# A four-block transformer on one core: stripes filled without DRAM, values copied by ScalarE, softmax buffers chosen by need, and the best of twelve orders

## The chip, the core and the metric

The kernel runs on one core of a Trainium2 chip. The time is the device time of one execution in microseconds. The kernel before takes 1323.22 us, the median of three runs (1322.68 to 1323.9). All numbers and matmul operands are 32-bit floats. A core has five engines with queues of their own: TensorE (PE; its weight loads are shown apart, as PEld), VectorE (DVE), ScalarE (ACT), GpSimd (POOL) and SyncE (SP), which here does nothing but issue DMAs.

## What is computed

Eight batches of 512 tokens by 256 features go through four residual blocks, each fed by a layer norm without gain or bias:

1. Attention of 16 heads of 16 features with rotary positions. Keys and values come from a latent of 64 features. A fixed bias by distance is added to the scores before the softmax, and a small gated term is added after it:

```python
q = apply_rope(x @ Wq + bq);  k, v = split((x @ Wkv_down + bkv_down) @ Wkv_up + bkv_up);  k = apply_rope(k)
att = softmax(q @ k.T / sqrt(16) + log_sparse + log(decay + 1e-9))
out = att @ v + 0.2 * sigmoid(q @ mean(k)) * mean(v)
x = x + out @ Wo + bo
```

2. A feed-forward block, 256 to 1024 to 256, with ReLU.
3. A retention block without softmax: `(q k^T * D) v`, with D = 0.96875^(i-j) on and below the diagonal.
4. The same feed-forward block again.

## The kernel before

Everything stays on chip: weights are loaded once, and each batch of x is loaded into one tile `x_b`. PE's work falls into two kinds.

*Steps.* The attention of one batch is 4 groups of 4 heads; each group has 8 items (4 blocks of 128 tokens by 2 pairs of heads), 32 items a batch and 256 in all. Item n appears three times. As a score item (`score_item`, tile `s`) it gives two heads' scores, 128 queries by 512 keys each, into a pair buffer of PSUM (tag `sc`, two buffers of two banks); VectorE takes the row maximum (`reduce_item`, tile `mr`). After eight items `shift` transposes the group's maxima (`mx`), ScalarE negates them (`neg`) and a DMA puts them into a spare row of the query tile, so that the next product subtracts them by itself. LAG steps later the item returns as a probability item (`prob_item`, tile `t`): the transposed scores, less the maxima. `soft_item` applies the exponential on ScalarE (tile `p`, four buffers) and multiplies by the decay table `dec_a` on VectorE or on POOL. Items below EARLY (34) put `t` into two of the three small banks (tag `m`) and take two exponentials of 512 columns; later ones take the pair buffer and one of 1024. PVLAG (2) steps later, every second step, `pv_item` multiplies by the values.

Score and probability matmuls use a 32-row strip of the PE array per head: the tiles `qT` and `kT` hold head h of each group in a stripe of 32 partitions, 16 rows of features, one row for the shift, the rest zeros or ones. Both exist twice, for even and odd batches.

*Units.* All other work is cut into `Unit`s, each a function with an estimated PE time, the engines that follow and their times (`then`), predecessors (`after`), and the first step at which it may go. `front1` and `front2` make the units of a batch before its attention: layer norm (`ln_units`: statistics, 1/sigma on POOL, normalization, transposition `xT`), the latent (`lat`), keys, queries, values (`va`), the means for the gated term (`km`, `mv`, `me`, `ga`). Keys and queries come out of PSUM on VectorE as products with cosine and sine (`half_unit`, tiles `rc` and `rs`); `turn` (L446) adds them on POOL, writes them to the DRAM tiles `dk` and `dq`, and reads them back with one DMA for each head of a group, which gives the stripes their order. The values are written by four VectorE additions that also add their bias (L383). `post_units` divides by the softmax's sums; for batches 1 to 6 it goes through DMAs and a reciprocal (`invert`, `divide`), with planned delays of 4.5 and 5.8 us. `rest` makes the units of the output product (`wo`), the two feed-forward blocks (`up`, `down`, tiles `h_x`/`hx` and `x`) and the retention block (`b`, `bv`, `bs`, `bo`).

*The order.* Instructions are pinned to the program order on each engine. The first batch's front is written out by hand from L814. From L835 a planner runs the rest: it keeps clocks for PE, VectorE, ScalarE and POOL, the times at which PSUM buffers come free, and at each turn either issues the next step or a unit from one of the waiting chains. A unit is taken when the next step would leave PE idle, when the chains' backlog is over RESERVE (75 us), and as far as a credit that shares the remaining unit work among the remaining steps allows it. LAG is 10. All loads and stores go through SP's queue in program order; only the shift's DMA goes through ScalarE's.

Of the kernel before, what the change touches and what calls it, by code (L numbers as in the profile page):

```python
# [15 lines left out]
P = 128  # L16
# [19 lines left out]
def tile_kernel(  # L36
# [70 lines left out]
    for h in range(2):  # L107
        move(xs[0][:, 2 * h : 2 * h + 2, :], xv[0][:, 2 * h : 2 * h + 2, :])
# [7 lines left out]
    for j in range(2):  # L116
        move(wd_sb[:, :, j, :], wdown)

    wk_in = at.tile([P, NH, 32], F32, tag="p", bufs=4, name="wk_in")
    for j in range(2):  # L120
        move(wk_in[j * LAT : (j + 1) * LAT].rearrange("p h d -> p (h d)"), wk[:, 0, :])
    wq_in = at.tile([P, NC, NH, 32], F32, tag="p", bufs=4, name="wq_in")
    move(wq_in.rearrange("p c h d -> p c (h d)"), wq[:, :, 0, :])
# [4 lines left out]
    for j in range(2):  # L128
        move(wv_sb[j * LAT : (j + 1) * LAT], wv)
    row = keep([P, 2, D], "row")  # L130
    move(row[:, 0, :], rows[0:D].partition_broadcast(P))
    move(row[:, 1, :], rows[2 * D : 3 * D].partition_broadcast(P))
    wqk_in = rs.tile([P, NC, 2, D], F32, tag="big", bufs=1, name="wqk_in")
    move(wqk_in, wb[:, :, 0:2, :])
    bv, b2 = row[:, 0, :], row[:, 1, :]
    move(vec[LAT:, V_BD : V_BD + 1], vecs[:LAT, V_BD : V_BD + 1])
# [10 lines left out]
    dq = [dr.tile([NH, HD, T], F32, tag=f"dq{i}", name=f"dq{i}") for i in range(2)]  # L147
    dk = [dr.tile([NH, HD, T], F32, tag=f"dk{i}", name=f"dk{i}") for i in range(2)]
# [11 lines left out]
    def buffers(i, eng):  # L160
        eng.memset(kT[i], 1.0)
        eng.memset(qT[i], 0.0)
        gps.memset(vaug[i], 1.0)

    def head_mask():
        dve.reduce_sum(hmask, ident.rearrange("p (h d) -> p h d", d=HH), axis=AX.X)
        gps.tensor_scalar(hmask, hmask, 0.5 / T, None, ALU.mult)
        gps.memset(kmean, 0.0)

    def memory_buffers():  # L170
        for i in range(2):
            gps.memset(gates[i], 0.0)
            move(gates[i][NH : NH + 1, :], rope[HD : HD + 1, 0, :])
            gps.memset(mem[i], 0.0)
        gps.memset(bo_row, 0.0)
        move(bo_row[NH : NH + 1, :], rows[D : 2 * D].unsqueeze(0))
        move(bvc, rows[0:D].rearrange("(c p) -> p c", p=P))
        gps.memset(vmean, 0.0)
        gps.memset(vmask, 0.0)
        gps.memset(vmask[:, :, NH : NH + 1], 1.0)  # L180
        for c in range(NC):
            dve.reduce_sum(
                vmask[:, c, c * HH : (c + 1) * HH], ident.rearrange("p (h d) -> p h d", d=HD), axis=AX.X
            )
        gps.tensor_scalar(bvc, bvc, 0.1, None, ALU.mult)

    late = {}

    def late_loads():
        late["dec_a"] = resident(decay_a, "dec_a")  # L190
        xs[1] = load_x(1)

        for g in range(NG):
            at_row = (g % 2) * 4 * HD
            move(wo_sb[at_row : at_row + 4 * HD, g // 2, :], wo.rearrange("(h d) g n -> h d g n", d=32)[:, :HD, g, :])
        late["w1"] = resident(w1, "w1_sb")
        late["w2"] = resident(w2, "w2_sb")

        move(wvu[:, :, :D], wb[:, :, 2, :])
# [13 lines left out]

    wq_sb = keep([P, NC, 2, P], "wq_sb")

    wk_sb = keep([P, P], "wk_sb")
    def regroup():
        for e in range(2):
            half_of = slice(e * HH, (e + 1) * HH)
            act.copy(  # L220
                wk_sb[e * LAT : (e + 1) * LAT, :].rearrange("p (h d) -> p h d", d=HH),
                wk_in[e * LAT : (e + 1) * LAT, :, half_of],
            )
        for e in range(2):
            half_of = slice(e * HH, (e + 1) * HH)
            for c in range(NC):
                act.copy(wq_sb[:, c, e, :].rearrange("p (h d) -> p h d", d=HH), wq_in[:, c, :, half_of])
# [4 lines left out]
    def biases():  # L232
        pick = keep([P, 2, 32], "pick")
        for e in range(2):
# [3 lines left out]
            )  # L238
        ps = misc("qk_bias")
# [6 lines left out]
    NI = B * NG  # L246
    NS = 8 * NI
    LAG, PVLAG = 10, 2
# [19 lines left out]
    def product():  # L268
        ps = misc("ct")
        for c in range(NC):  # L270
            for o in range(NC):
                mm(ps[:, c * D : (c + 1) * D], wr[1][:, o, c * P : (c + 1) * P], wr[0][:, o, :], o == 0, o == NC - 1)
        dve.tensor_copy(ct.rearrange("p c d -> p (c d)"), ps)

    def product_biases():
        both = rs.tile([P, NC], F32, tag="ve", name="both")
        dve.tensor_mul(both, vec[:, V_BQB : V_BQB + NC], vec[:, V_BKB : V_BKB + NC])
        ones = rs.tile([P, P], F32, tag="xn", name="ones")
        gps.memset(ones, 1.0)
        ps = misc("bb")  # L280
        for j, v in ((0, V_BKB), (1, V_BQB)):
            for c in range(NC):
                for o in range(NC):
                    mm(
                        ps[:, 2 * j + c : 2 * j + c + 1], wr[j][:, o, c * P : (c + 1) * P], vec[:, v + o : v + o + 1],
                        o == 0, o == NC - 1,
                    )
        for o in range(NC):
            mm(ps[:, 4:5], ones, both[:, o : o + 1], o == 0, o == NC - 1)
        dve.tensor_copy(bb, ps[:, :5])  # L290
        dve.tensor_copy(wvu[:, :, D], bb[:, 2:4])
# [23 lines left out]
    def ln_units(get, name, pool, bias=None):  # L315
# [39 lines left out]
        for h in range(2):  # L355
            a = Unit(lambda h=h: stats(h), then=(("DVE", 1200), ("POOL", 1000)))
# [802 lines left out]
```

## Time and profile before

| | us |
|---|---|
| Median of three runs | 1323.22 |
| Profiled execution, its own time | 1321.83 |
| Its span, first to last instruction | 1320.0 |
| TensorE busy | 1241.8 (94%) |
| VectorE busy | 798.4 (60%) |
| ScalarE busy | 444.9 (34%) |
| GpSimd busy | 407.7 (31%) |
| Mean granted TensorE clock | 0.979 |

The chain that ended last lies on PE for 81% of the span and on VectorE for 13%. Three things are needed to read the profile. A float32 matmul shows as two passes, so a count of 1024 stands for 512 matmuls. Matmuls on different strips of the array overlap, so the mean duration of one (664 ns for `s`) is more than its share of busy time (297.4 us over 1024). And almost every instruction is issued through one helper for its engine, so lines say little (L69 for VectorE, ScalarE and POOL, L205 for matmuls, L91 for SP's DMAs) and the names of the tiles identify the work.

### The profile page before, as it was taken

Reading aid. Unit: us, or ns where it says so; the run is one execution under the profiler, and the core shown is the slowest. Engines: PE = TensorE matmul, PEld = TensorE weight load, DVE = VectorE, ACT = ScalarE, POOL = GpSimd, SP = SyncE. Lnnn points to the kernel's source line nnn. Section 1 sums busy time; section 2 is a strip of 40 time slices with the busy share of each in tenths; the row PEclk is TensorE's granted clock in tenths of the full one; section 3 lists DMA queues with packets and bytes.
Section 4 is the critical chain, followed back from the end, with each engine's and each line's share of the span. In section 5 each row is a group of like instructions: output and inputs, shape, how many; then the busy total and the mean of one; then the engine's idle time right before and its main releaser. Section 6 shows DMA issues by size and latency. Waiting matters only on the chain.

```text
span 1320.0 us, 15524 instructions
## 1 busy us (share of the span) xinstructions
PE 1241.8 (94%) x5972; PEld 609.7 (46%) x5972; DVE 798.4 (60%) x1300; ACT 444.9 (34%) x634; POOL 407.7 (31%) x461
## 2 busy tenths in 40 slices
PE   6899887989999999989999999999989999999999
PEld 3333232435452554435543455435535454555757
DVE  4587986687666576755766757565665465442320
ACT  2144434433434233332343423333233423332120
POOL 4165454243323233231332333232331223121210
PEclk9599999999998999999999999999989999999999
DMA  5440040022000400022000400013000000000000
GB/s 136 134 75 7 1 86 14 6 49 50 14 5 6 94 21 9 5 53 52 24 5 3 84 29 14 5 31 68 5 9 5 22 9 1 1 17 1 0 4 28
DMA packets 33935, 39.03 MB, mean 30 GB/s; under 512 B 11691, under 2 KB 21292, under 8 KB 33582
## 3 DMA queue, kind: packets, MB, share of 16 engines
q1 hardware_dynamic: 33222, 37.79, 12.4%
q8 instruction: 47, 0.77, 0.2%
q10 hardware_dynamic: 640, 0.26, 0.1%
q14 instruction: 26, 0.21, 0.1%
HBM read 21.65 MB, written 12.78 MB: 26 GB/s over the span
## 4 chain that ended last, share of the span: by engine, by line
PE 81%; DVE 13%; DMA 1%; issue 1%; ACT 1%; POOL 1%; SPq 0%; ACTq 0%; DVEq 0%
PE s L205 18%; PE x L205 17%; PE hx L205 16%; PE pv L205 7%; DVE mr L69 6%; PE wo L205 3%; PE bs L205 3%; DVE p L69 3%; PE bo L205 3%; PE t L205 3%; PE bv L205 2%; PE b L205 2%; PE q L205 1%; PE lat L205 1%; PE ga L205 1%
## 5 line engine op out<-in xcount | busy, mean ns | idle before, releaser
L69 ACT ACTIVATE p<-t 128x1024 f32<-128x1024 f32 (+1 forms) x290 | 264.1, 924 | 540.9 <-PE t L205 494.4
L69 DVE TENSOR_REDUCE mr<-s 128x2 f32<-128x1024 f32 x256 | 312.5, 1222 | 219.7 <-PE t L205 202.5
L69 POOL TENSOR_TENSOR p<-p,dec_a 128x512 f32<-128x512 f32 x182 | 233.3, 1302 | 464.5 <-ACT p L69 397.4
L205 PE MATMUL s<-kT,qT 32*128 32x512 f32 x1024 | 297.4, 664 | 40.0 <-DVE mr L69 35.3
L205 PE MATMUL t<-qT,kT 32*128 32x512 f32 x1024 | 298.2, 649 | 6.1 <-DVE mr L69 5.9
L69 DVE TENSOR_TENSOR p<-p,dec_a 128x512 f32<-128x512 f32 x330 | 231.5, 743 | 23.5 <-ACT p L69 23.2
L205 PE MATMUL x<-w_sb,h_x 128*128 128x256 f32 x1024 | 236.9, 387 | 4.6 <-DVE rs L69 4.6
L205 PEld LDWEIGHTS x<-w_sb,h_x 128*128 128x128 f32 x1024 | 194.3, 193 | 58.7 <-issue 26.9
L205 PEld LDWEIGHTS s<-kT,qT 32*128 32x128 f32 x1024 | 81.5, 189 | 215.2 <-DVE mr L69 101.2
L205 PE MATMUL pv<-p,va 128*32 128x512 f32 x1024 | 148.1, 609 | 3.0 <-DVE p L69 2.7
L69 ACT ACTIVATE h_x<-hx,vec 128x512 f32<-128x512 f32 x128 | 88.0, 688 | 142.3 <-PE hx L205 142.3
L205 PE MATMUL hx<-xT_g,w_sb 128*128 128x512 f32 x256 | 121.6, 613 | 0.7 <-ACT xT_g L69 0.7
L69 DVE TENSOR_TENSOR x<-x,x 128x256 f32<-128x256 f32 x64 | 27.1, 424 | 155.2 <-PE x L205 155.2
L205 PE MATMUL hx<-xT_f,w_sb 128*128 128x512 f32 x256 | 117.9, 601 | 1.9 <-ACT xT_f L69 1.8
L205 PEld LDWEIGHTS t<-qT,kT 32*128 32x128 f32 x1024 | 80.8, 185 | 24.6 <-DVE mr L69 9.2
L205 PEld LDWEIGHTS hx<-xT_g,w_sb 128*128 128x128 f32 x256 | 46.2, 192 | 68.6 <-issue 66.5
L205 PEld LDWEIGHTS hx<-xT_f,w_sb 128*128 128x128 f32 x256 | 45.9, 190 | 60.8 <-issue 52.3
L69 POOL TENSOR_TENSOR x<-x,row 128x256 f32<-128x256 f32 x64 | 47.8, 767 | 51.6 <-DVE xn_f L69 30.6
L205 PEld LDWEIGHTS pv<-p,va 128*32 128x32 f32 x1024 | 22.8, 108 | 80.2 <-issue 40.2
L69 POOL TENSOR_TENSOR rc<-rc,rs 128x512 f32<-128x512 f32 x32 | 43.8, 1390 | 15.1 <-DVE rs L69 15.1
L205 PE MATMUL bs<-xT_r,ret 128*128 128x512 f32 (+3 forms) x128 | 37.2, 440 | 0.0
L69 DVE COPY ret<-bv 128x257 f32<-128x257 f32 x32 | 13.1, 423 | 39.3 <-PE bv L205 39.3
(134 smaller groups left out, 976.0 us busy)
## 6 DMA issues: line engine op xcount, KB each, us to landing
dk<-rc SPq DMA_DIRECT2D x16, 256.0 KB
kT<-dk SPq DMA_DIRECT2D x32, 128.0 KB
dq<-rc SPq DMA_DIRECT2D x16, 256.0 KB
qT<-dq SPq DMA_DIRECT2D x32, 128.0 KB
out_dram<-x SPq DMA_DIRECT2D x32, 128.0 KB
x<-in_x_dram SPq DMA_DIRECT2D x7, 512.0 KB
aT<-num SPq DMA_DIRECT2D x96, 32.0 KB
rec<-d_rec SPq DMA_DIRECT2D x12, 256.0 KB
```

Of the source, the lines that this page charges most:

```text
L69: ins = f(*a, **k)
L205: tc.keep_in_program_order(nc.tensor.matmul(o, lhsT=l, rhs=r, start=start, stop=stop))
```

## The change

- **Stripes.** The DRAM tiles `dq` and `dk` go. Each rotated half (128 partitions: 16 heads by 8 features) is written by one DMA for each group straight into every fourth partition of `qT` or `kT`; the feature rows of a stripe are now its even rows, and the shift row is its row 1. `turn` issues eight such DMAs of 64 KB for keys and eight for queries.
- **Values.** Two ScalarE copies take the values out of PSUM without their bias. Since each row of the softmax sums to one, the bias of the values passes through `Wo` once and is added to `bo_row`.
- **Softmax items.** Below EARLY, an item takes the two small banks only where the plan's time for that is over 0.2 us earlier than the pair buffer's.
- **The first batch's front**, written by hand, has another order: the latent in two halves, `wq` loaded through ScalarE's queue, the next x and the decay table loaded ahead of the stripes, matmuls of the identity (`warm`) at the start and between score-only steps, the bias products of the retention block moved from PE to POOL and ScalarE, and part of the gate's and memory's units moved behind the first scores.
- **The planner** becomes a function that can run without emitting; it is run for four values of `reserve` and three of `later` (which shifts how much work is left for the tail), and the order with the lowest planned end is emitted. The planned end is charged 1.7 us for each planned gap on PE of more than 1.2 us. Several planned times change, among them the delays of the division (7.5 and 12 us), and 6 us for the stripes to land. LAG becomes 12.

```diff
-                move(d[:, e * HH : (e + 1) * HH, :], o)
-            src = d.rearrange("(g s) r t -> s r g t", s=4)
-            to = (qT, kT)[j][b % 2]
-            for h in range(4):
-                move(to[h * 32 : h * 32 + HD], src[h])
+        def stripes(j, g, e):
+            move((qT, kT)[j][b % 2][2 * e : P : 4, g, :], rot[j, e][g * 32 : g * 32 + 32, :])
...
+                rotate(j, e, gps)
+                for g in range(NG):
+                    stripes(j, g, e)
+            if j == 0 and b > 1:
+                move(qT[b % 2][1:P:32], zero_rows)
...
-                for i in range(2):
-                    dve.tensor_tensor(
-                        vaug[b % 2][:, 2 * i + j, : NH * 17].rearrange("p (h d) -> p h d", d=17)[:, :, :HD],
-                        ps[j][:, i * D : (i + 1) * D].rearrange("p (h d) -> p h d", d=HD),
-                        bv.rearrange("p (h d) -> p h d", d=HD),
-                        ALU.add,
-                    )
+                act.copy(
+                    vaug[b % 2][:, j::2, : NH * 17].rearrange("p i (h d) -> p i h d", d=17)[:, :, :, :HD],
+                    ps[j].rearrange("p (i h d) -> p i h d", i=2, d=HD),
+                )
...
+        def bias_through_wo():
+            ps = misc("bo")
+            for c in range(NC):
+                mm(ps[:, :D], vmean[:, c, :], wo_sb[:, c, :], c == 0, c == NC - 1)
+            dve.tensor_add(bo_row[: NH + 1, :], ps[: NH + 1, :D], bo_row[: NH + 1, :])
...
+    RESERVES, LATERS = (45000, 60000, 75000, 90000), (-30000, 0, 30000)
-    LAG, PVLAG = 10, 2
+    LAG, PVLAG = 12, 2
...
-        if n < EARLY:
+        if spare[n]:
...
-        u = [Unit(evacuate, then=(("ACT", 600), (None, 4500)))]
+        u = [Unit(evacuate, then=(("ACT", 600), (None, 7500)))]
-            u.append(Unit(invert, then=(("DVE", 350), (None, 5800)), after=u[-1:]))
+            u.append(Unit(invert, then=(("DVE", 350), (None, 12000)), after=u[-1:]))
...
+    latent(0, 2), latent(1, 2)
+    regroup_k()
+    regroup_q(1)
+    half_unit(0, 0, projected(0, 0))
+    k_ps = [projected(1, e) for e in range(2)]
+    half_unit(1, 0, k_ps[0]), half_unit(1, 1, k_ps[1], "sc")
+    rotate(1, 0, gps), rotate(1, 1, gps)
+    half_unit(0, 1, projected(0, 1), "sc")
+    rotate(0, 1, dve), rotate(0, 0, dve)
+    for g in range(NG):
+        for j, e in ((1, 0), (1, 1), (0, 1), (0, 0)):
+            stripes(j, g, e)
...
+            both = max(own, sc[need - 1] if need else 0)
+            if len(ts) == 1 and s is not None and ts[0] < EARLY:
+                apart = max(own, sc[0], banks[1])
+                if apart + 200 < both:
+                    spare[ts[0]], both = True, apart
...
+        between = {t: [Unit(lambda: warm(2), 500)] for t in (1, 3, 5, 7)}
+        between[9] = [ga0]
+        for j, t in enumerate((0, 2, 4)):
+            between[t] = [Unit(lambda j=j: bias_products(j), then=(("POOL", 1300), ("ACT", 1300)))]
+        for t in range(LAG):
+            step(t)
+            for u in between.get(t, []):
+                issue(u)
...
+        return clock["PE"] + 1700 * sum(g > 1200 for g in gaps)
+    rules = [(reserve, later) for reserve in RESERVES for later in LATERS]
+    cost = {r: plan(*r) for r in rules}
+    plan(*min(rules, key=cost.get), emit=True)
```

## The prediction

> **What bounds the kernel now.** I read the clock and span first (1320.0 us, granted clock 0.979), then the stretches, the chain by time, the time line, and last the waits. The stretches show where TensorE isn't used:
>
> ```profile
> 0.00:50.00 50.00, 33.99 (x134) 16.66 (x136) 25.40 (x46) 8.01 (x21) 18.62 (x37) 0.83 0.67 173
> 50.00:100.00 50.00, 45.87 (x201) 16.38 (x198) 36.85 (x47) 17.06 (x35) 23.42 (x22) 0.89 0.29 59
> 100.00:200.00 100.00, 90.66 (x503) 32.91 (x505) 84.33 (x115) 43.45 (x76) 51.64 (x46) 1.00 0.14 29
> 200.00:300.00 100.00, 88.91 (x482) 36.16 (x476) 73.56 (x108) 40.92 (x54) 36.65 (x36) 0.98 0.12 27
> 300.00:400.00 100.00, 97.85 (x490) 46.91 (x486) 65.32 (x120) 37.16 (x49) 31.79 (x40) 1.00 0.09 19
> ...
> 1100.00:1200.00 100.00, 96.65 (x446) 52.07 (x445) 41.31 (x78) 34.87 (x47) 25.66 (x29) 1.00 0.02 6
> ```
>
> The columns are length, PE, PEld, DVE, ACT, POOL busy, clock, DMA share, GB/s. From 300 us TensorE is busy 96 to 98 in 100: feed-forward matmuls fill whatever softmax leaves. Of the 78.3 us in which PE does nothing, 20.1 lie before 100 us, 20.4 between 100 and 300, 37.7 after. Where no feed-forward work exists yet (up to about 200 us) VectorE is the limit: one softmax step costs it a maximum of 1.22 us and half of a decay product of 1.28 us, 1.86 us, against 1.07 + 0.53 us of PE (scores with probabilities; values).
>
> The start, in the chain by time and then the time line:
>
> ```profile
> 24.53 2.46 POOL rc L69 x2
> 27.04 1.12 PE ga L205 x2
> ...
> 34.15 3.27 DMA qT<-dq
> 37.46 13.83 PE s L205 x27
> ```
> ```profile
> 22.14 1.80 SPq L91 DMA_DIRECT2D dk<-rc  x2
> 26.47 1.74 SPq L91 DMA_DIRECT2D kT<-dk  x4
> 28.31 1.17 SPq L91 DMA_DIRECT2D dq<-rc  x2
> 34.15 1.72 SPq L91 DMA_DIRECT2D qT<-dq  x4
> 42.54 1.23 DVE L69 TENSOR_REDUCE mr<-s 128x2 f32<-128x1024 f32 x1 [0.78 <-PE s L205]
> 47.93 1.23 DVE L69 TENSOR_REDUCE mr<-s 128x2 f32<-128x1024 f32 x1 [0.76 <-PE s L205]
> 63.47 0.70 PE L205 MATMUL t<-qT,kT 32*128 32x512 f32 x2
> ```
>
> The rotated queries are ready at 27.0 us; two DMA hops through DRAM on one in-order queue bring them to the stripes 10.4 us later. PE stands still, and its clock falls:
>
> ```profile
> 33.00:36.00 3.00, 0.00 (x0) 0.00 (x0) 1.30 (x1) 0.00 (x0) 1.28 (x2) 0.56 0.32 83
> 39.00:42.00 3.00, 3.00 (x9) 1.18 (x8) 1.23 (x1) 0.00 (x0) 0.00 (x0) 0.50 0.98 302
> 57.00:60.00 3.00, 3.00 (x9) 1.54 (x6) 1.62 (x3) 0.00 (x0) 0.00 (x0) 0.50 0.01 3
> 60.00:63.00 3.00, 2.32 (x9) 1.20 (x7) 0.41 (x1) 0.59 (x1) 0.00 (x0) 0.89 0.00 0
> ```
>
> From 36 to 60 us the clock is 0.50 although PE is busy, so a score item takes 2.0 us where a step of the steady part issues scores and probabilities in 1.07; even VectorE waits 0.76 us for each. The first probabilities start at 63.5 us.
>
> **The change, part by part.** The sum is made against the profiled execution: 1321.8 us, 1.8 more than its span and 1.4 less than the median of the runs (1323.2).
>
> *Up to the first score.* Removed: both hops, and the gate and memory units from the front of the chain. The latent goes by halves, so its first half no longer waits for the second transposition; wq goes on ScalarE's queue, and the weight copies no longer stand ahead of the xT copies (10.30 to 11.20 us). POOL gets about 4 us of memsets ahead of the first 1/sigma, so normalization gains nothing. Second xT half at about 11.7; 1.0 us of latent matmul; the first query half (1.9 us) to 14.5; keys to 15.6. VectorE then makes eight rope products of 0.66 us: key products to 18.5, query to 19.8. POOL adds the keys (1.25 us each) by 20.3, VectorE the queries by 21.3. The four stripes of group 0 cost about 0.59 us of SP each (the SBUF-to-SBUF row, aT<-num, median 587 ns); the last issue ends near 22.3, and landing takes the 1.6 us that qT<-dq took after its last issue. First score 24 us. Ends: 23 (no contention between POOL and VectorE) to 29 (x_1 and the decay table, 0.96 MB now ahead of the stripes, at the 200 GB/s of 12 to 15 us are 4.8 us in the way). I take 24: these loads would be issued by 16 us.
>
> *A rule about small transfers* speaks against stripes. The row is 587 ns of issue for 32 KB. The Trainium skill, DMA: Bandwidth & Descriptors, section Bandwidth, says transfers under 64 KB are dominated by descriptors and puts one of 64 KB at 0.95 us. By the row sixteen stripes take 9.4 us, by that estimate 15.2; group 3 would come 6 us later, still ahead of its first item, so the sum is the same.
>
> *Score-only steps.* Twelve instead of ten (eleven were issued before the first t). At full clock VectorE sets the pace: 12 x 1.25 us, plus about 1.5 us for the gate matmuls and four warming pairs (0.5 us of PE each). First probabilities at 24 + 0.9 + 15 + 1.5 = 41.4, against 63.5: **-22.1**. The shift (transposed maxima, copy, DMA) of items 0 to 7 has four items, 5 us, to hide in. If the clock stays at half speed, twelve items cost 2.03 us each, 9.4 us more: first probabilities at 51.
>
> *The clock rule.* In the trace, matmuls on 32 rows alone didn't bring the clock back in 20 us; it returned after 128-row ones (me at 57.99, tr_a at 59.86). The Trainium skill, TensorE: Matmul & The Clock Gate, section Part 1: The HAM clock gate, says about 3.4 us of sustained work releases the throttle; by that page it would have been back near 41 us, so the measurement decides. By the page the warming pairs would be needless and the sum no better.
>
> *Displaced work.* Batch 1's normalization, transpositions and latent lay inside the old score-only time. They move into a stretch bound by VectorE: 2 x (0.74 + 0.30 + 0.73) + 0.41 = **+3.9** us there; their 4.1 us of PE cost 0 to 4.1, I take **+2.0**. One item more is done when probabilities start: **-1.9**.
>
> *Values by ScalarE.* Four VectorE additions (1.41 us a batch, 182.66 us) become two ScalarE copies (0.58 us each, by xT_f). VectorE binds for batch 1 alone: **-1.4**. Elsewhere 0: ScalarE is busy 34%. Behind each copy wait the next exponentials; uncovered, 7 x 1.17 = 8.2 us lost. The bias through wo adds one product of four matmuls and one addition (1.1 us PE, 0.4 DVE) once, beside VectorE's waits: 0 to +1.1, taken 0.
>
> *Stripes in the steady part.* Each batch issues 16 x 0.587 = 9.4 us on SP for 12 issues, 5.5 us, and 5.5 us of waits for dk and dq (22.4 and 21.9 us over 8 batches). SP is otherwise idle, the planner grants 6 us for landing, and both tensors are double buffered: 0. Out DMAs, x loads and reciprocal rows queued behind get no later. Without the cover, the 10 us would meet the first scores of a batch; ends -5 to +5.
>
> *Softmax placed by need.* Items below 34 always used two small banks and two exponentials (0.60 us each); now the pair buffer and one of 1.02 us unless the small banks are 0.2 us earlier. ScalarE gains 5.8 us that hide behind VectorE: 0. Against it, a pair buffer is freed by the maximum: PE's waits for it are 35.3 us in 50, 0.71 each; all 34 items: +24. I take 0.
>
> *Twelve orders.* After 200 us 48.8 us are idle and the clock loses 13.8 (sum of 1 less the clock over its 20 us stretches). One stall shows what new figures remove:
>
> ```profile
> 584.52 0.68 SPq L91 DMA_DIRECT2D rec<-d_rec  x1
> 588.43 0.69 DVE L69 TENSOR_TENSOR aT<-aT,rec 128x512 f32<-128x512 f32 x1 [9.05 <-DMA rec<-d_rec]
> 590.50 6.70 PE L205 MATMUL x<-w_sb,h_x 128*128 128x256 f32 x16 [4.59 <-DVE rs L69]
> ```
>
> The division was placed 5.8 us after the inversion and its rows came 8.2 us after d_rec's issue; the new figure is 12. PE lost 4.59 idle and 6.70 - 3.70 at low clock, 7.6 us. A new order brings stalls of its own, so I take half, **-4**. Ends: -30 (half of all 62.6) to +20, a third more of them.
>
> Sum: 1321.8 - 22.1 + 3.9 + 2.0 - 1.9 - 1.4 - 4 = 1298.3, with 1.4 for the median about **1300**.
>
> **The rivals.** (a) *The start gains half*: the clock stays at 0.5 through the scores (+9.4) or the stripes land late (+5). For it: 24 us at 0.50 above. Against: 128-row matmuls fill the time ahead and every second step. 1305 to 1315. (b) *The order is much better*: 15 to 30 us of the 62.6 are found instead of 4: 1274 to 1289. For it: five drops of the clock after 200 us, which the planner now charges 1.7 us each; against: it still compares sums of rounded durations. (c) *Slower*: early probabilities wait in the pair buffers for VectorE's maxima. At 177.23 and 185.25 us, where they already share, PE waits 1.23 and 0.96 us for them. At 1.1 us for all 34 items it costs 37 us, 1337. It outweighs the gain of 23.5 from 21 items on. Against: the separate banks are kept where the plan sees 0.2 us. (d) *Nothing comes of it*: the head start is given back where batch 1 waits for its front, since all displaced work sits there: 1323.
>
> **How the numbers follow.** The forecast (1288 to 1312) has 0.52, (a) beyond it 0.17, (b) 0.13, (c) 0.14, (d) 0.04. The range of 1276 to 1324 leaves out most of (c) and the far end of (b), 0.17 together. A difference of 0.2%, 2.6 us, is about what a measurement of this kernel can tell from none. Faster is the first three, 0.82; (d) is same, 0.04; (c) slower, 0.14.
>
> **What would show it.** First score near 24 us and first probabilities near 41, with a clock of 1.00 in 25 to 45 us; PE idle in the first 100 us near 10 instead of 20.1; no DMA into or out of dk and dq; va written by ScalarE in 0.6 us; no division waiting over 5 us; VectorE above 85% busy from 45 to 180 us. I am wrong if scores start later than 29 us, if the clock stays at 0.5 while they run, if PE's waits for maxima before 200 us grow by over 20 us, or if PE's idle time after 200 us grows from 48.8 to 70.

## The result, and the profile after

The changed kernel takes 1310.81 us, the median of four runs (1306.07 to 1314.41), against 1323.56 before (1322.68 to 1328.34) on the same chip. The ratio is 0.9894 [0.985, 0.9938]: faster by 12.7 us, where 23 were forecast. The profiled execution took 1313.35 us with a span of 1311.6 and a granted clock of 0.969.

The stretches of the changed kernel, as they were shown for before (length; PE, PEld, DVE, ACT, POOL busy; clock; DMA share; GB/s), with one more for 400 to 1000 us:

```profile
0.00:50.00 50.00, 38.54 (x179) 20.82 (x179) 26.95 (x40) 12.51 (x36) 17.60 (x35) 0.86 0.57 163
50.00:100.00 50.00, 43.35 (x222) 14.12 (x222) 37.85 (x53) 19.23 (x29) 22.66 (x22) 0.86 0.03 9
100.00:200.00 100.00, 84.36 (x429) 30.08 (x427) 68.31 (x97) 36.63 (x53) 46.84 (x46) 0.83 0.10 27
200.00:300.00 100.00, 88.78 (x478) 34.86 (x476) 71.22 (x108) 42.07 (x56) 33.80 (x37) 0.97 0.06 15
300.00:400.00 100.00, 93.35 (x484) 46.38 (x483) 71.70 (x112) 35.47 (x46) 36.40 (x39) 1.00 0.10 27
400.00:1000.00 600.00, 589.52 (x2945) 286.89 (x2945) 396.44 (x628) 223.13 (x301) 191.20 (x212) 1.00 0.08 21
1100.00:1200.00 100.00, 92.78 (x409) 52.43 (x408) 34.80 (x70) 29.79 (x40) 20.45 (x22) 0.95 0.02 6
```

Set against the lines of before, two things stand out. From 100 to 200 us the new kernel is worse: TensorE is busy 84.4 us instead of 90.7, at a clock of 0.83 instead of 1.00, and VectorE too does less, 68.3 against 84.3. From 400 to 1000 us it is better: 589.5 us busy where before had 576.9:

```profile
400.00:1000.00 600.00, 576.87 (x2813) 279.04 (x2812) 385.03 (x620) 211.32 (x283) 184.74 (x206) 0.98 0.13 29
```

The time line of the start, with the instructions that set the first score:

```profile
6.20 6.50 SPq L91 DMA_DIRECT2D b<-in_rows_dram  x1
13.38 0.64 SPq L91 DMA_DIRECT2D b_row<-in_vecs_dram  x1
14.70 0.36 DVE L69 COPY wq_sb<-wq_in 128x128 f32<-128x128 f32 x2 [6.62 <-DMA wq_in<-in_wq_dram]
15.07 3.45 PE L201 MATMUL q<-xT_a,wq_sb 128*128 128x512 f32 x4 [4.99 <-DVE wq_sb L69]
22.20 0.34 SPq L91 DMA_DIRECT2D b_rows<-b_row  x1
22.58 0.43 SPq L91 DMA_DIRECT2D x<-in_x_dram  x1
23.06 0.50 SPq L91 DMA_DIRECT2D dec_a<-in_decay_a_dram  x1
24.76 1.19 SPq L91 DMA_DIRECT2D kT<-rc  x2
28.98 0.47 SPq L91 DMA_DIRECT2D qT<-rc  x1
31.08 1.48 PE L201 MATMUL s<-kT,qT 32*128 32x512 f32 x8 [3.22 <-DMA qT<-rc]
52.16 2.05 PE L201 MATMUL t<-qT,kT 32*128 32x512 f32 x4
```

wq lands late (its copies wait for it until 14.70 us), SP is held for 6.5 us by the load of b, and then sits from 14.0 to 22.2 us in front of b_rows, because that load reads back from DRAM what b_row is only just writing there. x_1, the decay table and the stripes are queued behind it. The first score comes at 31.1 us (37.5 before) and the first probabilities at 52.2 (63.5 before).

The clock in the same three-microsecond stretches as before, and then the time line where batch 1 begins:

```profile
33.00:36.00 3.00, 2.86 (x12) 1.41 (x10) 1.96 (x3) 1.56 (x8) 1.52 (x2) 0.50 0.42 107
39.00:42.00 3.00, 3.00 (x14) 1.39 (x8) 1.74 (x2) 0.00 (x0) 0.00 (x0) 0.50 0.19 60
57.00:60.00 3.00, 3.00 (x16) 1.76 (x12) 1.73 (x2) 1.08 (x2) 0.39 (x1) 0.50 0.00 0
```
```profile
135.92 4.93 SPq L91 DMA_DIRECT2D qT<-rc  x8
140.54 1.22 PE L201 MATMUL s<-kT,qT 32*128 32x512 f32 x2 [6.07 <-DMA qT<-rc]
142.66 1.23 DVE L69 TENSOR_REDUCE mr<-s 128x2 f32<-128x1024 f32 x1 [9.11 <-PE t L201]
```

Batch 1's stripes are issued from 135.9 us. Its first score waits 6.07 us for them, and VectorE stands 9.11 us. Before had no such wait.

**Where the head start went.** At the moment at which the exponentials of softmax item k start, one can take the time elapsed less the TensorE work issued so far, each matmul pass that the trace shows counted at what it takes at full clock with nothing in its way (0.134 us for one of scores or probabilities, 0.43 us for one of 512 columns on the full array, and so on; the warming products, whose values are used nowhere, as nothing). What is left is TensorE time lost so far, in us, worked out from the records of the profiled executions; the last column is the whole span less the whole work, so what is lost behind the last item is its difference to k=256. The table also has six of the experiments below:

| kernel | k=1 | 16 | 32 | 64 | 96 | 128 | 160 | 192 | 224 | 256 | end |
|---|---|---|---|---|---|---|---|---|---|---|---|
| before | 34.9 | 48.0 | 60.4 | 80.9 | 95.3 | 103.1 | 121.2 | 131.5 | 145.5 | 151.4 | 159.8 |
| changed | 28.9 | 43.3 | 68.0 | 87.1 | 103.4 | 113.5 | 120.0 | 125.3 | 129.7 | 137.1 | 151.8 |
| e5, before with stripes | 31.6 | 44.7 | 57.0 | 77.5 | 92.0 | 99.7 | 115.3 | 126.2 | 140.8 | 146.9 | 155.3 |
| e6, old delays | 29.5 | 42.8 | 64.5 | 80.4 | 90.1 | 95.9 | 110.1 | 122.1 | 129.5 | 134.2 | 148.8 |
| e7, head of ten | 31.7 | 50.3 | 65.2 | 88.4 | 102.1 | 109.6 | 118.8 | 124.3 | 131.6 | 136.2 | 142.8 |
| e8, start put right | 20.0 | 33.5 | 55.8 | 74.3 | 90.7 | 100.7 | 107.3 | 112.6 | 116.9 | 124.4 | 139.3 |
| e9, old planner | 30.1 | 44.1 | 55.7 | 72.1 | 91.0 | 104.3 | 114.5 | 121.3 | 126.4 | 135.3 | 150.0 |
| e11, rule (60000, 30000) | 30.5 | 42.9 | 67.6 | 90.4 | 108.1 | 116.2 | 127.1 | 142.0 | 148.1 | 160.1 | 179.6 |

The changed kernel is 6.0 us ahead at the first probabilities, 7.6 us behind at item 32 (batch 1's start), and 10.4 behind at item 128. Then before loses 42 us from item 128 to 224 and the changed kernel 16, so that it is 14.3 us ahead at item 256. Behind the last item it loses 14.7 us and before 8.4, so it gives 6.3 back. Each row is one execution. Those of before and of the changed kernel are 8.4 us apart where the medians are 12.7 apart: the changed kernel's profiled execution is 2.5 us slower than its median.

### The profile page after: what moved, and what is told of

Its sections match the earlier page's. It is cut to its first block, busy times and chain, and to the rows that moved or that the text cites. A ratio compares the mean times of both kernels' runs of the same rounds, so it can differ in the third digit from the quotient of the medians.

```text
span 1311.6 us, 15603 instructions
## 1 busy us (share of the span) xinstructions
PE 1233.7 (94%) x6002; PEld 606.6 (46%) x6002; DVE 792.7 (60%) x1269; ACT 455.1 (35%) x634; POOL 408.6 (31%) x463
## 4 chain that ended last, share of the span: by engine, by line
PE 82%; DVE 12%; DMA 2%; issue 1%; SPq 1%; POOL 1%; ACT 1%; DVEq 0%; POOLq 0%; ACTq 0%
PE s L201 18%; PE x L201 17%; PE hx L201 17%; DVE mr L69 7%; PE pv L201 7%; PE wo L201 3%; PE bo L201 3%; PE bs L201 3%; PE b L201 2%; PE bv L201 2%; DVE p L69 2%; PE t L201 2%; SPq L91 1%; PE ga L201 1%; PE lat L201 1%
## 5 line engine op out<-in xcount | busy, mean ns | idle before, releaser
L69 POOL TENSOR_TENSOR p<-p,dec_a 128x512 f32<-128x512 f32 x182 | 230.1, 1285 | 460.2 <-ACT p L69 400.1
L69 DVE TENSOR_TENSOR p<-p,dec_a 128x512 f32<-128x512 f32 x330 | 227.4, 730 | 25.9 <-ACT p L69 25.8
L201 PE MATMUL x<-w_sb,h_x 128*128 128x256 f32 x1024 | 233.9, 384 | 0.0
L201 PEld LDWEIGHTS s<-kT,qT 32*128 32x128 f32 x1024 | 79.1, 190 | 227.3 <-DVE mr L69 122.1
L201 PE MATMUL hx<-xT_g,w_sb 128*128 128x512 f32 x256 | 118.2, 604 | 0.8 <-ACT xT_g L69 0.7
L69 POOL TENSOR_TENSOR x<-x,b 128x256 f32<-128x256 f32 x64 | 50.3, 805 | 49.3 <-DVE xn_f L69 27.3
L201 PE MATMUL q<-xT_a,wq_sb 128*128 128x512 f32 x64 | 32.4, 636 | 5.6 <-DVE wq_sb L69 5.0
L201 PE MATMUL bs<-xT_r,ret 128*128 128x512 f32 (+3 forms) x128 | 37.5, 441 | 0.0
```

The costliest lines, as they stand in the source:

```text
L69: ins = f(*a, **k)
L201: tc.keep_in_program_order(nc.tensor.matmul(o, lhsT=l, rhs=r, start=start, stop=stop))
```

## The experiments

Theory 1, the prediction's, was that a head start is carried to the end. Its rival was that it is absorbed where VectorE or batch 1's preparation sets the pace, and that what was won in the end was won by the order of the rest. The kernel before was run anew beside each group: 1322.96 us (e1 to e4), 1325.21 (e5 to e8), 1322.48 (e9 to e12). Ratios are to those. The changed kernel itself was not measured again beside them, so a comparison with it goes from one group to another, and those groups ran on different chips.

### e1: three loads in two halves

```
-    move(wk_in.rearrange("p h d -> p (h d)"), wk[:, 0, :].unsqueeze(0).to_broadcast([2, LAT, NH * 32]))
+    for j in range(2):
+        move(wk_in[j * LAT : (j + 1) * LAT].rearrange("p h d -> p (h d)"), wk[:, 0, :])
```
(and the same for bd and wv_sb)

> Only three weight loads at the start differ from the changed kernel: bd, wk_in and wv_sb are each loaded by two DMAs of 64 partitions, as before the change, and not by one DMA whose source is broadcast over a first dimension of 2. Theory 1 (the broadcast loads use two of the sixteen DMA engines; the DMA share in the changed kernel falls to a tenth from 5 to 6 us, and wq lands behind them at 14.7 us): wq lands near 10 us as it did before, PE's wait of 4.99 us for the wq copies falls below 1 us, SP's 6.5 us issue of b below 1 us, the first score comes near 26 us instead of 31.1, and 4 to 6 us of that reach the end: 1305 to 1307. Theory 2 (wq is late because ScalarE's queue issues it at 5.26 us and a second queue shares the same engines): wq still lands after 13 us, nothing changes by more than 1 us at the start, 1310 to 1311.

1309.34 us (1305.26 to 1312.38), ratio 0.9897 [0.9859, 0.9936]. The time line of this kernel:

```profile
8.10 0.58 SPq L91 DMA_DIRECT2D b<-in_rows_dram  x1
9.36 0.62 SPq L91 DMA_DIRECT2D b_row<-in_vecs_dram  x1
13.39 0.36 DVE L69 COPY wq_sb<-wq_in 128x128 f32<-128x128 f32 x2 [5.27 <-DMA wq_in<-in_wq_dram]
19.50 0.34 SPq L91 DMA_DIRECT2D b_rows<-b_row  x1
22.57 1.57 SPq L91 DMA_DIRECT2D kT<-rc  x2
29.94 2.09 PE L204 MATMUL s<-kT,qT 32*128 32x512 f32 x8 [4.90 <-DMA qT<-rc]
```

Loading both halves in one broadcast had a price: b is now issued in 0.58 us instead of 6.50, and wq_sb's copies start 1.3 us sooner. The Trainium skill, DMA: Bandwidth & Descriptors, section Why a DMA increments its semaphore by 16 and not by 1, says that a transfer uses the largest number of engines, up to 16, that divides the slowest dimension (other than 1) of both its source and its destination; the broadcast's slowest dimension is 2, and this run agrees, though it doesn't show the number of engines. But the first score came only 1.1 us sooner, not the 5 of the first theory: SP still waits, 9.4 us, for b_row's way through DRAM, and the stripes are still behind it. The time can't be told from the changed kernel's 1310.81. The late loads were one cause of two, and not the one that ended last.

### e2 and e3: batch 1's layer norm early

```
+        for t_ in (3, 4, 5, 6, 7, 8):
+            between.setdefault(t_, []).append(chains[2].pop(0))
```
e2 is the changed kernel with this; e3 has e1's loads too.

> The six layer-norm units of batch 1 (statistics, normalization, transposition) are issued between the score-only steps 3 to 8, as the order before the change had them, and not from step 12 on; all else is planned as in the changed kernel. Theory 1 (the head start is lost because batch 1's front starts late: PE waits 6.07 us for its query stripes at 134 to 140 us, and the clock falls with it): the wait for the stripes falls below 1 us, the score-only steps become 2 to 4 us longer, and the end comes 6 to 12 us earlier, 1299 to 1305. Theory 2 (the stretch up to 200 us is bound by VectorE, and its 3.5 us of layer norm cost the same wherever they stand): the wait goes, but the first probabilities are later by as much and the end moves by less than 3 us, 1308 to 1313.

> Both edits: the three loads by two DMAs each, and batch 1's layer norm between the score-only steps. If both first theories hold the gains add, because one shortens the time up to the first score and the other a wait 100 us later: 1293 to 1301, below both single edits by 4 us or more. If what is gained ahead is absorbed by a later wait (the rival for the whole: the pace of VectorE up to 200 us decides), it is within 3 us of the better of the two.

e2: 1310.61 us (1309.2 to 1311.45), 0.9905 [0.9868, 0.9942]. e3: 1307.8 (1306.07 to 1307.96), 0.9884 [0.9854, 0.9915]. In e2 no score waits for batch 1's stripes any more, and the stretches from 120 us on show what stands in its place:

```profile
120.00:130.00 10.00, 9.08 (x61) 3.37 (x61) 7.62 (x14) 4.71 (x6) 6.01 (x8) 1.00 0.01 2
130.00:140.00 10.00, 6.85 (x48) 2.41 (x48) 8.77 (x12) 4.22 (x6) 5.67 (x5) 1.00 0.00 0
140.00:150.00 10.00, 6.76 (x48) 1.81 (x46) 9.36 (x14) 4.17 (x6) 5.93 (x6) 1.00 0.01 2
```

From 130 to 150 us VectorE (the third of the busy times) has 8.8 and 9.4 us of 10, and TensorE (the first) under 7. By the same ledger as above, e2 loses 12.2 us from item 16 to 32 where the changed kernel loses 24.7, but it had lost 6.5 more by item 16, and 32 to 64 cost 5.7 more; at item 64 the two stand at 86.8 and 87.1. The 6.5 are not the layer norm's earlier place alone: in this execution the clock stood at 0.50 from 30 to 55 us. In e3, with the same order, it stayed at 1.00 until 45 us, and e3 is 1.5 us below e1 and 2.8 below e2, so the gains don't add to the 4 us that the first theory wanted. Taking the wait away gained nothing in the time that these runs can tell.

### e4: the values by VectorE again

```
-                act.copy(
+                dve.tensor_copy(
                     vaug[b % 2][:, j::2,
```

> The two copies of the values out of PSUM go to VectorE instead of ScalarE, still without bias; the planned times and so the order are those of the changed kernel. My account (VectorE binds for batch 1 alone, about 1.4 us for each batch in which it binds, hidden elsewhere): 1 to 3 us slower, 1311 to 1314. Rival (VectorE binds PE's waits in most batches, since PE's waits for maxima are 40 us in all): 5 us slower or more, 1316 to 1320. Second rival (the copies behind exponentials on ScalarE delay them): faster by 2 us or more.

1311.53 us (1309.94 to 1314.44), 0.9916 [0.9887, 0.9945]: no difference that this run can tell. This kernel has the start of the changed one, and its clock happened to stay at 1.00 from 30 to 50 us, where the changed kernel's fell to 0.50. From its first score (31.33 us) to its first probabilities (51.13) it took 19.8 us; the changed kernel took 21.1.

### e5: before, with the stripes alone

```
-                move(d[:, e * HH : (e + 1) * HH, :], o)
-            src = d.rearrange("(g s) r t -> s r g t", s=4)
...
+                for g in range(NG):
+                    move(to[2 * e : P : 4, g, :], o[g * 32 : g * 32 + 32, :])
```

> The kernel before with one part of the change: each rotated group is written straight into its stripes and not through DRAM; order of work, values' copies and biases are those of before. The first score then waits for the last products of the rotation alone and should come near 33 us in place of 37.5, the first probabilities near 55 to 58 in place of 63.5. Theory 1 (a head start is carried): 4 to 10 us of the time are gone, 1313 to 1319. Theory 2 (the start is given back where batch 1 is prepared, since VectorE sets the pace there): the row maximum of item 48 comes at 174 to 177 us as before (176.0), and the time is within 3 us of before, 1320 to 1326.

1317.87 us (1314.19 to 1318.55), 0.9936 [0.9912, 0.9961]: 7.3 us faster. First score 32.8 us, first probabilities 59.7. In the table its lead over before is 3.3 at item 1, 3.3 at 16, 3.4 at 32, 64 and 128, and 4.5 at 256: carried to the end without loss. (The profiled executions are 4.5 us apart, the medians 7.3.) Theory 1 holds where the order is the same.

### e6: the division's old planned delays

```
-        u = [Unit(evacuate, then=(("ACT", 600), (None, 7500)))]
+        u = [Unit(evacuate, then=(("ACT", 600), (None, 4500)))]
-            u.append(Unit(invert, then=(("DVE", 350), (None, 12000)), after=u[-1:]))
+            u.append(Unit(invert, then=(("DVE", 350), (None, 5800)), after=u[-1:]))
```

> The changed kernel with the planned delays of the division as before (4.5 and 5.8 us in place of 7.5 and 12 us), the planner's rule held at the one that the changed kernel uses (75000, 0). Theory 1 (what was won from 400 to 1000 us is won by these delays): divisions wait again on VectorE, the row maximum of item 224 comes 8 to 20 us later than 960.6, and the time is 1319 to 1331. Theory 2 (the gain there comes from the softmax items placed by need): within 4 us of the changed kernel, 1307 to 1315.

1309.71 us (1305.53 to 1312.62), 0.9878 [0.9849, 0.9906]. Its waits of VectorE over the whole span, as in before and unlike the changed kernel, have divisions waiting for their rows (total, times, longest); and its stretches from 200 us:

```profile
DVE aT L69 <- DMA rec<-d_rec: 8.9, 3, 4.9
```
```profile
200.00:400.00 200.00, 190.78 (x1003) 83.48 (x995) 145.26 (x225) 81.55 (x108) 68.01 (x75) 1.00 0.07 18
400.00:1000.00 600.00, 577.02 (x2879) 282.82 (x2877) 389.11 (x617) 215.88 (x291) 188.71 (x209) 0.99 0.08 22
```

This answers the question in an unexpected way. From 400 to 1000 us TensorE falls back to 577.0 us busy, what before had: in this order the new delays make that stretch fuller, and they remove the division's waits. (In e11 below, with the new delays and another rule, it has 576.3.) But from 200 to 400 us this kernel is busy 190.8 us, the changed one 182.1. What the delays win late they lose early, and the time is the same. A gain read off one stretch of one order was not a gain.

### e7: a head of ten items

```
-    LAG, PVLAG = 12, 2
+    LAG, PVLAG = 10, 2
```

> The changed kernel with the scores 10 items ahead of the probabilities in place of 12, as the kernel before had it. Theory 1 (the longer head lets batch 1's preparation be displaced, and keeps the banks filled): the first probabilities come about 4 us sooner, batch 1's stripes are late by more or fewer items, and from 400 to 1000 us waits for the row maxima come back, 1315 to 1325. Theory 2 (the length of the head is paid back and changes nothing): within 4 us of the changed kernel, 1307 to 1315.

1305.37 us (1304.44 to 1307.16), 0.9849 [0.9827, 0.9871]. Neither theory: it is at least as fast as the changed kernel, perhaps 4 us faster than e6 of the same group. The planner chose its order anew. First score 31.7 us; first probabilities 55.1, not sooner, with the clock at 0.50 from 35 to 55 us. In the table it stands where the changed kernel stands at item 256 (136.2 and 137.1), and then loses 6.6 us where that loses 14.7. Of the kernels in the table those with a head of ten lose 6.6 to 8.4 us behind the last item, those with twelve 14.6 to 19.5. So the longer head isn't what makes the changed kernel faster; by these rows it costs it some 6 to 8 us at the end.

### e8: the start put right

```
-        xs[1] = load_x(1)
-        late["dec_a"] = resident(decay_a, "dec_a")
...
     def late_loads():
+        xs[1] = load_x(1)
+        late["dec_a"] = resident(decay_a, "dec_a")
...
-        move(wr["rows"][:, 0:2, :], b_row.unsqueeze(0).to_broadcast([P, 2, D]))
...
             stripes(j, g, e)
+        if g == 0:
+            move(wr["rows"][:, 0:2, :], b_row.unsqueeze(0).to_broadcast([P, 2, D]))
```
(with e1's loads; `loads_before_scores()` stands ahead of `bias_rows()`)

> The changed kernel with its start put right: the two-part loads of the earlier run, and the loads of x_1 and of the first decay table and the bias row's way back from DRAM issued only after the first group's stripes. No wait for the bias row is left ahead of the stripes on SP's queue; stripes are issued near 18 us and the first score comes at 24 to 27 us (31.1 in the changed kernel). Theory 1 (a head start is carried one to one): 4 to 6 us less, 1303 to 1307. Theory 2 (it is absorbed by the wait for batch 1's stripes and VectorE's work between 100 and 200 us, as it was from before to after): the row maximum of item 48 stays at 174 to 177 us and the time within 3 us of the changed kernel, 1308 to 1313.

1302.56 us (1299.88 to 1305.07), 0.983 [0.98, 0.986]: faster than before by 22.7 us, and by its ratio and its four times faster than the changed kernel (of another group). Its time line and its clock:

```profile
20.05 1.73 SPq L91 DMA_DIRECT2D kT<-rc  x2
22.50 0.54 SPq L91 DMA_DIRECT2D qT<-rc  x1
23.14 1.19 SPq L91 DMA_DIRECT2D b_rows<-b_row  x1
25.75 1.14 PE L204 MATMUL s<-kT,qT 32*128 32x512 f32 x8 [1.23 <-DMA qT<-rc]
44.43 1.13 PE L204 MATMUL t<-qT,kT 32*128 32x512 f32 x4 [0.30 <-DMA qT<-neg]
```
```profile
30.00:35.00 5.00, 5.00 (x26) 2.24 (x24) 4.43 (x5) 1.50 (x7) 1.62 (x2) 1.00 0.54 148
35.00:40.00 5.00, 5.00 (x20) 1.88 (x17) 4.46 (x4) 0.27 (x1) 0.00 (x0) 1.00 0.86 284
```

With nothing in front of the stripes the first score is at 25.75 us and the first probabilities at 44.43, at full clock and with VectorE busy nine tenths of the time. Its order is the changed kernel's, and its lead over that in the table is 8.9 us at item 1, 12.2 at 32, 12.8 at 64 and at 128, 12.7 at 256. It grew where batch 1 begins, then stayed to a tenth. It still waits 7.65 us for batch 1's stripes at 128.4 us. Theory 1 again, and beyond its number: 7 us less than e6 and 8 less than the changed kernel, where 4 to 6 were expected. The 12.5 us of the table's last column are more than that, because the changed kernel's profiled execution lies 2.5 us above its median and this one's 1.7 below.

### e9: the old planning on the new start

```
-                t += 100 if shape[0] != "U" else 0
-            at_ += 90 if shape[0] == "U" else 0
-                    landed[u.gives[1]] = t + 6000
+                    pass
-                if apart + 200 < both:
-                    spare[ts[0]], both = True, apart
+                spare[ts[0]], both = True, apart
...
```
(and the durations, the delays and the needs of before)

> The changed kernel (its start, its values by ScalarE, its head of 12 items) with the planning of before: no charge for the change between units and softmax steps, no 6 us for the stripes' landing, no wait of an item for the item before it, the old planned durations and delays, items 0 to 33 always in the small banks, and the rule held at (75000, 0). Theory 1 (what the changed kernel gains after 200 us is gained by the planner's new figures): TensorE's lost time between 200 and 1260 us goes from 73 back to 83 to 90 us, as it was before (87) and with stripes alone (85), and the time is 1318 to 1328. Theory 2 (the loss after 200 us follows from the start and the head, or scatters from order to order whatever the figures are): 66 to 78 us lost there, 1304 to 1315.

1310.87 us (1310.08 to 1313.62), 0.9917 [0.9897, 0.9938]: theory 2. The planner's new figures, the placing of the early items by need and the delays, all undone together, change nothing in the time, and TensorE's lost time between 200 and 1260 us is 76 us (73 in the changed kernel, 87 in before). It keeps the head of twelve items and the handwritten order of the first twelve steps. In the table this kernel is 15 us better than the changed one at item 64 (it has no late batch 1), 9 better at 128, and 2 better at 256. The planning moves waits from one stretch to another.

### e10: no warming pairs

```
-        between = {t: [Unit(lambda: warm(2), 500)] for t in (1, 3, 5, 7)}
+        between = {t: [Unit(lambda: None, 500)] for t in (1, 3, 5, 7)}
```

> The changed kernel without its four warming pairs between the twelve score-only steps, order otherwise the same; only those warming products are left out, whose values are used nowhere. Theory 1 (the warming pairs keep or bring back TensorE's clock): the clock stays at 0.50 until after 50 us as in the kernel before, the first probabilities come 3 to 9 us later than 52.2, and the time is up to 6 us longer, 1311 to 1318. Theory 2 (they come too rarely to matter, 0.5 us of every 4): first probabilities within 2 us of 52.2 and the time 1306 to 1313.

1312.05 us (1310.15 to 1313.78), 0.9925 [0.9901, 0.995]: no difference in the time that this run can tell. First probabilities 54.8 us, a little past theory 2's two microseconds. Three kernels with the same start and with the warming pairs have 54.5 (e9), 54.9 (e11) and 51.1 (e4). In e9 the clock stood at 0.50 from 35 to 50 us as it did here, pairs and all.

### e11: another of the twelve orders

```
-    RESERVES, LATERS = (45000, 60000, 75000, 90000), (-30000, 0, 30000)
+    RESERVES, LATERS = (60000,), (30000,)
```

> The changed kernel with its order held at the rule (60000, 30000), which the planner puts at 1298.2 us against 1264.2 for the one it chooses, 34 us worse. Theory 1 (the planner's figure tells orders apart): 15 to 35 us slower than the changed kernel, 1325 to 1345. Theory 2 (its ranking is not followed by the chip): within 8 us of it, 1303 to 1319.

1341.6 us (1339.34 to 1343.33), 1.0145 [1.0124, 1.0166]: slower than the changed kernel by 31 us, where the planner said 34. Its waits of TensorE, and those of the changed kernel, over the whole span:

```profile
PE s L201 <- DVE mr L69: 49.6, 65, 3.1
PE t L201 <- DVE mr L69: 5.5, 4, 2.2
```
```profile
PE s L201 <- DVE mr L69: 40.4, 61, 2.4
PE t L201 <- DVE mr L69: 4.4, 3, 1.7
```

The order does matter, then, and for this pair of orders the planner's figure sees the difference. The comparison itself still wins nothing over before: the lowest of the twelve planned ends (1264.2 us, the planner's figure and no time of the chip) belongs to (75000, 0), the constants that before had.

### e12: the right start and batch 1 early

e8 with e2's edit.

> The kernel with its start put right (first score 25.7 us, 1302.6) and with batch 1's layer norm taken up between the score-only steps 3 to 8. TensorE waited 7.7 us there for batch 1's stripes at 128 us. Theory 1 (that wait is time on the path): the wait goes and 4 to 7 us with it, 1295 to 1299. Theory 2 (VectorE sets the pace until 200 us, as in the earlier run where this move was absorbed): the row maximum of item 64 stays within 3 us of 220.1 and the time 1300 to 1304.

1306.76 us (1306.04 to 1308.87), 0.9885 [0.9866, 0.9905]: slower than e8, as neither theory had it. The time line of this kernel says why, and below it one line of its stretches:

```profile
31.47 0.58 SPq L91 DMA_DIRECT2D x<-in_x_dram  x1
35.50 0.75 DVE L69 BATCH_NORM_STATS2 st_a<-x 128x6 f32<-128x256 f32 x2 [4.03 <-DMA x<-in_x_dram]
38.48 1.23 PE L207 MATMUL tr_a<-ident,xn_a 128*128 128x128 f32 x4 [5.18 <-DVE xn_a L69]
```
```profile
35.00:40.00 5.00, 1.52 (x8) 1.05 (x10) 4.34 (x8) 0.85 (x4) 1.63 (x3) 0.64 0.84 250
```

x_1 is now loaded after the stripes, from 31.5 us. Its layer norm, put early, makes VectorE wait 4.03 us for it, with the maxima of the scores queued behind; TensorE runs dry and its clock falls to 0.64 to 0.68 until 55 us. First probabilities 55.2 us. Each edit can be made alone; together they get in each other's way.

## Why the prediction was right or wrong

*The whole.* Forecast 1300 in a range of 1276 to 1324, measured 1310.8: the sign and the range were right, the gain was a little over half of the forecast one. The time lies in the place of rival (a), 1305 to 1315, and still inside the forecast's own 1288 to 1312. Two of the four signs of being wrong came true: the scores started later than 29 us, and the clock stood at 0.50 while they ran. The other two did not: PE's waits for maxima before 200 us grew by 8.4 us, and its idle time after 200 us is 44 us. PE's idle time in the first 100 us is 18.1 us, where near 10 was named. That the sum came as near as it did is in part luck: the head start was undone by item 32, and what came in its place, -20.5 us between items 64 and 256, was forecast at -4 and for another reason.

*Up to the first score: the step that failed first.* "I take 24: these loads would be issued by 16 us." They were issued at 22.6 and 23.1, because SP sat behind b (6.5 us) and then 8.1 us in front of b_rows. Neither wait was costed, although the diff shows a write to b_row and a read of it on the same queue ahead of the stripes. The upper end, 29, priced only the transfer of x_1 and the table, and the first score came at 31.08. wq's late landing was missed as well: the first query product ran from 15.07 to 18.5 us, and was to end at 14.5. e8, without these waits, has 25.75.

*Score-only steps.* The forecast was 17.4 us from the first score to the first probabilities. At full clock it is 18.7 (e8) to 19.8 (e4); the changed kernel took 21.1 and e9 24.5. So the term was sized right but for 1 to 2 us, and the two whose clock fell took 1 to 6 us more, not the 9.4 of the rival. Of the step's -22.1, -11.3 came (63.47 to 52.16); 7.1 of the missing 10.8 is the late first score, 3.7 the longer score-only time.

*The clock.* The prediction expected 1.00 from 25 to 45 us. It was 0.50 from 33 to 42 and 1.00 in e8 and e4. The warming pairs, which it thought the measured rule made useful, made no difference that can be told (e10). Its reading that matmuls on 32 rows alone left the clock down for 20 us isn't quite the trace's: four passes on the full array (tr_a, 1.12 us from 51.22 us) lay among them and didn't bring it back either.

*Displaced work.* +3.9 and +2.0 were forecast. From item 16 to 32 the changed kernel loses 24.7 us, before 12.4: 12.3 in place of 5.9. The prediction costed the work and not its date: batch 1's stripes came after its first score was due. That mechanism stands in rival (d), with a chance of 0.04, and by the table it did undo the head start; only the total of (d) was wrong, since the order won elsewhere.

*VectorE.* It was to be more than 85% busy from 45 to 180 us; it was busy 94.2 of 135 us, 70% (81% before). TensorE's clock (0.82 over that stretch, 0.94 before) and the wait for batch 1 took the rest. With the wait gone (e2) VectorE does bind from 130 to 150 us, as the prediction read it from before.

*Costed at nothing, and right:* the stripes in the steady part (scores wait for stripes twice in all, at the first score and at batch 1; eight of them took SP 4.93 us, 0.62 each, where 0.59 was taken); the softmax by need (6 of the 34 early items are split into the small banks, and up to 200 us TensorE waits for maxima 2.9 us ahead of probabilities and 12.9 ahead of scores, before 7.4 in all, so that rival (c) with its 37 us falls; e9 says the same). The bias through wo was also put at nothing, and no run has it alone. The values at -1.4 can't be told from nothing (e4).

*The order.* -4 was forecast, for half of the division's stall. The table gives -20.5 between items 64 and 256 and +6.3 behind the last item, about -14. The +6.3 has no term in the prediction, which saw the head of twelve only at its beginning (one item more done, -1.9); e7 points to that head. The named stall did go, but it isn't the cause: with it back (e6) the time is the same, and with all of the old planning back (e9) it is the same too.

*What is shown and what stays open.* The stripes alone are worth 7.3 us, over half of the gain. The other 5 or so did not go away when the delays, the planner's figures and the early items' placing (e9), the values (e4) or the warming pairs (e10) were taken back. What is left is the rest of the new start; that it is the cause is argued by what was left over and not shown. With it every order here loses less from item 128 to 224 than before's order does: 22 to 34 us (e7, e9, e11, e6; 16 in the changed kernel), against 42. That alone makes no fast kernel, since e11 is among them. Why the order of before does so much worse there was not found. The bias through wo was not tried alone, nor e8's start with e7's shorter head, which the two results suggest as the next kernel.

## What to carry to other kernels

A head start was worth its full length here when the order of the rest stayed (e5, e8: from item 32 to 128 the lead was the same to 0.1 and to 0.6 us), and when the order changes with it, the two must be measured apart, for a planner moves waits from stretch to stretch and the fuller stretch proves nothing. For a load moved ahead of a critical transfer, look at what its queue waits for, not only at its bytes: here a 2 KB row that went through DRAM held the queue, and the stripes behind it, for 8 us. And before a unit is put earlier, look when its inputs land, and who is queued behind it.

## What the runs showed of the hardware

Score matmuls on 32 rows didn't by themselves lower the clock. In e8 they ran at 1.00 from 26 us to 60, with TensorE busy 3.59 of the 5 us ahead of 30; in the changed kernel it was busy 2.13 of those 5, and the clock then fell:

```profile
25.00:30.00 5.00, 2.13 (x10) 1.44 (x8) 0.74 (x2) 2.74 (x7) 0.00 (x0) 1.00 0.75 237
30.00:35.00 5.00, 3.79 (x18) 1.80 (x18) 2.36 (x2) 0.91 (x4) 3.44 (x6) 0.68 0.36 93
35.00:40.00 5.00, 5.00 (x20) 2.15 (x16) 2.36 (x2) 1.50 (x7) 0.84 (x2) 0.50 0.33 86
40.00:45.00 5.00, 5.00 (x24) 2.55 (x20) 4.44 (x4) 0.00 (x0) 0.00 (x0) 0.80 0.68 211
```

The length of the pause ahead of the first score sorts these runs better than the busy time. After 1.23 us (e8) and 2.46 (e4) the clock stayed at 1.00; after 3.22 us (the changed kernel) and more (3.50 to 4.90 in e9, e11, e7, e6, e2 and e1) it fell every time; in between, it fell after 2.90 (e10) and not after 3.09 (e3). But a pause isn't needed. In e5 the clock fell at 33.4 us with TensorE busy in every microsecond from 28 to 34, behind 20 matmul passes of one column (the 16 below and four more from 32.30 us):

```profile
30.60 1.84 PE L203 MATMUL bb<-vec,wr 128*128 128x1 f32 x16
32.82 1.62 PE L203 MATMUL s<-kT,qT 32*128 32x512 f32 x8
33.00:34.00 1.00, 1.00 (x8) 0.13 (x7) 0.97 (x2) 0.00 (x0) 1.00 (x2) 0.68 0.42 107
```

That these passes are the reason was not tried. The kernel before has them too, just ahead of its own fall at 33 to 36 us. Once down, the clock stayed at 0.50 for some 10 us in the changed kernel (by the rows above) and for at least 15 us (35 to 50 us) in e9, e10 and e11, with TensorE busy all that time in e9 and e11. The Trainium skill, TensorE: Matmul & The Clock Gate, section Part 1: The HAM clock gate, has about 3.4 us of sustained work bring the clock back; these runs don't agree, and whatever counts as work there, score matmuls on 32 rows with a few full ones between them were not enough of it.
